# Seven-product attention: order of combine and denominators, place of one maximum, of the statistics and of the filling work

## Chip, cores and metric

The kernel runs on one core of a Trainium2 chip. The metric is device time in microseconds (us); a lower number is better. TensorE does the matmuls, VectorE (DVE in the profile), ScalarE (ACT) and GpSimd (POOL) the elementwise work, and SyncE (SP) starts most of the DMAs.

## What is computed

The input is four images of 256 channels and 64 x 64 pixels, in fp32. Two layers follow each other. The reference, cut to what matters:

```python
# layer 0: attention over the 4096 pixels of one image
q = wq @ x + bq            # 32 x 4096
k = wk @ x + bk            # 32 x 4096
v = wv @ x + bv            # 256 x 4096
attn = softmax(q.T @ k)    # 4096 x 4096, over the keys
x = gamma * (v @ attn.T) + x

# layer 1: cluster block, then MLP, then pointwise
y = x + ls1 * cluster(group_norm(x))   # 4 heads of 24, folds of 32 x 32, 4 centres each
y = y + ls2 * (W2 @ gelu(W1 @ group_norm(y)))          # 256 -> 1024 -> 256
z = relu(batch_norm(y * dw_w))
z = relu(batch_norm(pw_w @ z))
```

Group norm needs mean and variance over a whole image, and the cluster block needs sums of the attention's output over patches (the "cells").

## The kernel before, in words

**Stages.** The images go through one after the other: attention (some 495 us of an image's 800), cluster, MLP. Around them the work of the next image is interleaved: its projections, its first scores and the maxima of its first block of queries are made during the cluster block and the MLP of the image before. Only the first image has a stretch of its own for that, `alone` (L810), the prologue.

**Attention.** `weighting` (L880) goes over eight blocks of 512 queries; each block over eight units of 512 keys, so an image has 64 units, u = 8 nb + g. TensorE multiplies the 512 x 512 exponentials of a unit with v. In units g = 0 to 6 this is done with seven products in place of eight quarter products (`weigh`, L682: 28 matmuls of 128x256); the operands need sums of the four quarters of the exponentials (`factors`: VectorE makes t31 in L619, GpSimd the rest through `plus`, L598 and L614). Unit 7 is done plainly (L660). `weigh` is cut into four parts, and between the parts stand the pieces of other work: TensorE's order of work is thus written out by hand in this loop.

**Scores ahead.** `due` puts the scores of the unit eleven further on between the parts: two products (L423) into one buffer of two PSUM banks, a copy to SBUF (`kept`, ScalarE, L436) and a running maximum (`highest_of`, VectorE, L447), which reads the PSUM tile. There are two such buffers, but one of them holds the block's maximum and a part of the exponentials (`hold`) during the whole weighting. In a few places (`kept_only`, and the second half of a unit g = 0) the maximum isn't taken from PSUM but later from the SBUF copies: it is put into the list `held`, and `caught(n)` runs the first n of that list. In the trace the first kind reads `top<-sc,top`, the second `top<-s,top`.

**A unit on the other engines.** `exps(u+1)` subtracts the maximum (VectorE, L586, twice 128x1024) and takes exponentials (ScalarE, L591, L592, L595). `factors(u+1)` follows.

**End of a block.** With unit 7, `evict` copies the first two of the four accumulators out of PSUM (ScalarE, L702). `gather` sums the denominators (GpSimd, two additions of 128x256 into `rden`, L598). `combine` (L712 to L715) joins the copied quarters in four operations of 128x256; it runs on GpSimd in blocks 0 to 6 and on VectorE in block 7. `complete` (L727, VectorE) adds the other two accumulators to that, and only then may the next block's first matmul into them start. Later units of the next block do `total` (the denominators' reciprocal), `leave` (L751, the division, on GpSimd) and `sent` (DMA to a DRAM buffer). GpSimd's queue starts the DMAs that add the result to x (`back`, L775).

**Statistics.** Units 57 to 62 carry for each finished block two bn_stats (`seen`, L797) ahead of the first part of `weigh`, and the sum of the cells (`pooled`, L802) ahead of its third part, all on VectorE.

**Filling.** `cluster` (L1042) has many short dependent steps. Between them `fill(n)` pops n pieces from the list of the next image's projections: 32 halves of v (`v_half`, matmuls L378, ScalarE's copy L386) with four pieces for q and k among them (`halved`: matmuls, then two halves of the fp32 value made by ScalarE, L335, and VectorE, L336, and four stores each on SP's queue). `fill(N)` in `mlp` (L1842) takes all that are left, after the MLP's first piece.

Of the kernel before, what the change touches and what calls it, by code (L numbers as in the profile page):

```python
# [8 lines left out]
F32 = mybir.dt.float32  # L9
F32R = mybir.dt.float32r  # L10
# [4 lines left out]
P = 128  # L15
B, C, H, W = 4, 256, 64, 64
N = H * W
KC = C // P
NB = 512
NBLK = N // NB  # L20
# [9 lines left out]
RG, GRP = 4, N // NB  # L30
# [4 lines left out]
SEVEN = 7  # L35
# [18 lines left out]
def attention_then_cluster_block(  # L54
# [250 lines left out]
    def attention(b, xs, ys):  # L305
# [20 lines left out]
        def halves_of(which, i, hi, lo, ps, dma=nc.sync):  # L326

            col = 1 if which == "k" else 0
            if which not in own:
                own[which] = dram.tile([NBLK // RG, P, 4, NB], F32, tag=which, name=f"{which}_{b}")
            bias = bqk_s[:, col : col + 1]
            nc.scalar.activation(hi, ps, AF.Identity, bias=bias)  # L335
            nc.vector.scalar_tensor_tensor(  # L336
                lo, ps, bias, hi.bitcast(F32), ALU.add, ALU.subtract
            )
            rows = own[which][i]
            for c in range(4):  # L340
                part = hi if c in ((0, 2) if which == "k" else (0, 1)) else lo
                dma.dma_start(out=rows[:, c], in_=part.bitcast(F32))
# [16 lines left out]
        def halved(which, i):  # L359

            ps = ps_m.tile([P, NB], F32, tag="m", name=f"{which}p_{b}_{i}")
            parts = [
                big.tile([P, NB], F32R, tag="k", bufs=2, name=f"hl{j}_{which}_{b}_{i}")
                for j in range(2)
            ]
            projected(which, i, ps)
            halves_of(which, i, *parts, ps)

        vps = {}

# [17 lines left out]
        def v_pair(i):  # L388
            v_half(2 * i)
            v_half(2 * i + 1)  # L390
# [121 lines left out]
        def across(nb, tag="w2", tp=None):  # L512
            if tp is None:
                tp = turned_over(nb, ps_m.tile([P, 4, P], F32, tag="m", name=f"tt_{b}_{nb}"))
            mx = small.tile([P, 4], F32, tag="mx", name=f"mx_{b}_{nb}")
            nc.vector.tensor_reduce(mx, tp, AX.X, ALU.max)
            dg = work.tile([P, 4, P], F32, tag=tag, bufs=1, name=f"dg_{b}_{nb}")
            nc.vector.tensor_tensor(
                dg,
                ident.unsqueeze(1).to_broadcast([P, 4, P]),  # L520
                mx.unsqueeze(2).to_broadcast([P, 4, P]),
                ALU.mult,
            )
            return dg
# [267 lines left out]
                y = block(ys, k, nb).rearrange("p (h n) -> p h n", h=2)  # L792
                nc.vector.tensor_tensor(y, y, rows_of(t, k), ALU.add)

        def seen(nb):
            for c in range(KC):
                nc.vector.bn_stats(stats[:, 2 * nb + c, :], block(ys, c, nb))  # L797

        def pooled(nb):
# [12 lines left out]
        def alone():  # L812

            roots()
            for i in range(3):
                v_pair(i)
            staged("first", (("k", 0), ("q", 0)))
            k_unit(0)
            q_block(0)
            q_block(1)  # L820
            for i in range(3, 8):
                v_pair(i)
            for g in range(4):
                for f in sums(g):
                    f()
            for u in range(GRP):
                if u == 0:
                    begun(0)
                    staged("second", (("k", 1), ("q", 1)))
                    rest = load_rest()  # L830
                hooks, maxima = [], []
                score(u, hooks, maxima)
                for f in hooks + maxima:
                    f()
                v_pair(u + GRP)
                if u > 1:
                    next(rest, None)
            fold(0)
            for g in range(4, SEVEN):
                for f in sums(g):  # L840
                    f()
            dgs["dg"] = across(0)
            half(GRP, 0)
            spread(0, dgs["dg"])
            wf()
            half(GRP, 1)
            exps(0)
            factors(0)
# [32 lines left out]
        def weighting(next_x, fill, early, begin):  # L881
# [25 lines left out]
            for u in range(units):  # L907
                nb, g = divmod(u, GRP)
                more = nb + 1 < NBLK
                ripe = more and nb and g == 5  # L910

                short = nb == 0 and g == 6
                if g == 0:
                    done, av = av, [
                        pool.tile([P, NB], F32, tag=tag, name=f"av{c}_{b}_{nb}")
                        for c, (pool, tag) in enumerate(
                            ((ps_a, "a0"), (ps_a, "a1"), (ps_m, "m"), (ps_m, "m"))
                        )
                    ]
                maxima = due(u, 0)  # L920
                if g == GRP - 1:
                    gather(nb)
                if g == SEVEN:
                    evict(nb, av, 0)
                    evict(nb, av, 1)
                    combine(nb, nc.gpsimd if more else nc.vector)
                if g + 1 < GRP or more:
                    exps(u + 1)
                for f in maxima:
                    f()  # L930
                if nb < 2 or g == 3:
                    caught(1)

                if nb and g == 0:
                    complete(nb - 1, done, 1)
                elif nb and g == 1:
                    den = total(nb - 1)
                    next(den)
                elif nb and g == 2:
                    next(den)  # L940
                elif ripe:
                    peak = highest(nb + 1)
                    next(peak)
                if u == 0:
                    early()
                if u in views:
                    seen(views[u])
                if u in shifts:
                    shift(shifts[u])
                weigh(u, av, 0)  # L950
                if short:
                    two = ps_s.tile([P, 2, NB], F32, tag="s", name=f"tt_{b}_{nb + 1}")
                    tp = turned_over(nb + 1, two[:, 0].rearrange("p (j n) -> p j n", j=4))
                for f in due(u, 1):
                    f()
                weigh(u, av, 1)
                if short:
                    dgs["dg"] = across(nb + 1, "w2", tp)
                if g == GRP - 1 and not more:
                    complete(nb, av, 0)  # L960
                if u == units - 2:
                    back_one(NBLK - 2)
                maxima = due(u, 2)
                if more and nb and g == GRP - 2:
                    known(mb)
                if g + 1 < GRP or more:
                    factors(u + 1)
                if ripe:
                    next(peak)
                    mb = next(peak)  # L970
                for f in maxima:
                    f()
                if (u, 0) not in at or (u, 1) in at:
                    caught(1)
                if u in views:
                    pooled(views[u])
                weigh(u, av, 2)
                if short:
                    spread(nb + 1, dgs["dg"])
                for f in due(u, 3):  # L980
                    f()
                if nb and g == 1:
                    next(den)
                elif nb and g == (4 if more else 3):
                    leave(nb - 1)
                elif nb and g == (5 if more else 4):
                    sent(nb - 1)
                weigh(u, av, 3)
                if g == 3 and nb + 2 < NBLK:
                    q_block(nb + 2)  # L990
                if g == GRP - 1 and more:
                    complete(nb, av, 0)
                tail(u)
# [38 lines left out]
        parts.score, parts.fold, parts.q_block, parts.k_unit = score, fold, q_block, k_unit  # L1032
        parts.maximum, parts.first, parts.exps, parts.half = maximum, first, exps, half
        parts.projections = [lambda i=i: v_half(i) for i in range(N // P)]
        for i, f in (
            (27, lambda: halved("q", 1)),
            (20, lambda: halved("k", 1)),
            (14, lambda: halved("q", 0)),
            (13, lambda: halved("k", 0)),
        ):  # L1040
            parts.projections[i:i] = [f]
        return parts  # L1042


# [2 lines left out]
    def cluster(b, ys, stats, cells, rest, fill, gelu, nxt, maxima, turn):  # L1047
# [213 lines left out]
                        stop=(not first and j == 7),  # L1261
                    )

        fill(2)
        heads(NBLK - 1)
        similar(1)
        fill(2)
        summed(lambda j, q: pool_w[:, j], True)
        gelu(1)
        turn()  # L1270
        fill(4)
        table(AF.Sqrt)

        affine(0)
# [48 lines left out]
        )  # L1323
        g_s = work.tile([P, C], F32, tag="acc", bufs=1, name=f"g_{b}")
        nc.scalar.copy(g_s, gp[:, :C])
        fill(1)
        stats2 = small.tile([P, 2 * NBLK, 6], F32, tag="stats", name=f"st2_{b}")
        pieces = {}

# [59 lines left out]

        nxt.q_block(0)  # L1390
        nxt.k_unit(0)
        fill(4)
        copies = []
        nxt.score(0, copies, maxima)
        copies.pop()()
# [644 lines left out]
```

## Time and profile before

| | us |
|---|---|
| median of 3 runs | 3228.34 (3226.5 to 3228.45) |
| the profiled execution, its own time | 3225.25 |
| its span in the trace | 3223.3 |
| prologue, 0 to 74: TensorE busy | 51.99 of 74.00 |
| weighting of the first image, 74 to 569: TensorE busy | 477.94 of 495.00 |
| cluster of the first image, 569 to 633: TensorE busy | 57.08 of 64.00 |
| MLP of the first image, 633 to 870: TensorE busy | 234.83 of 237.00 |

The mean TensorE clock granted is 0.991 of full speed.

How to read the lines: an instruction or a group names its line in the code, engine, operation, and tiles as output<-inputs (buffer numbers left out) with partitions x elements. In the timeline a line begins with the start and the duration in us; in brackets at its end stands how long its engine was idle ahead of it and which instruction ended the idle time. In the list of groups the count is followed by the busy time, the mean duration of one in ns, and then the idle time ahead of the group's instructions with what ended it. In the list of waits each line has the waiting engine, its tile and line, then the one waited for, and the total, the number of times and the longest. A wait for several things is put down to the one that came last.

### The profile page before, as it was taken

How to read it: one execution, taken by the hardware profiler on the slowest of the kernel's cores; microseconds unless marked ns; L12 is line 12 of the kernel's file. 1: busy time of each engine (PE TensorE's matmuls, PEld its weight loads, DVE VectorE, ACT ScalarE, POOL GpSimd, SP SyncE). 2: the span in 40 equal slices, each digit the busy share in tenths (PEclk: the TensorE clock that was granted, in tenths of full speed). 3: DMA queues.
4: the chain of work that ended last, by engine and by line, in shares of the span. 5: the costliest groups of instructions: out<-in, count | busy, mean ns of one | idle time of the engine just before them, and what ended most of it. 6: DMA issues, size and time to landing. Idle time of an engine off the chain costs nothing.

```text
span 3223.3 us, 40475 instructions
## 1 busy us (share of the span) xinstructions
PE 3087.0 (96%) x13890; PEld 2444.0 (76%) x13890; DVE 2506.6 (78%) x3648; ACT 1732.9 (54%) x2719; POOL 2259.6 (70%) x2143
## 2 busy tenths in 40 slices
PE   7999999999999999999999999999999999998999
PEld 5777787688677787778867778776876787875786
DVE  4888887667788887777778888777778888877665
ACT  4556554545555656344555666544555556654444
POOL 4778787378488778647848878855766788783663
PEclk8999999999999999999999999999999999999999
DMA  5122116100112112510011211441011122150000
GB/s 163 40 63 63 54 58 188 63 20 30 46 50 63 53 60 87 160 50 21 30 56 43 63 60 58 112 126 50 30 43 43 53 59 63 56 142 7 14 20 27
DMA packets 105869, 200.33 MB, mean 62 GB/s; under 512 B 14416, under 2 KB 30400, under 8 KB 104128
## 3 DMA queue, kind: packets, MB, share of 16 engines
q1 hardware_dynamic: 101856, 181.94, 17.7%
q0 software_dynamic: 2976, 14.70, 2.5%
q8 instruction: 110, 1.80, 0.2%
q10 hardware_dynamic: 832, 1.11, 0.1%
q14 instruction: 95, 0.78, 0.1%
HBM read 149.37 MB, written 48.34 MB: 61 GB/s over the span
## 4 chain that ended last, share of the span: by engine, by line
PE 46%; POOL 26%; DVE 15%; issue 6%; ACT 4%; DMA 2%; SPq 0%; POOLq 0%; ACTq 0%; DVEq 0%
PE mo L1652 10%; PE av L682 9%; POOL acc L598 8%; PE hq L1735 5%; DVE top L447 4%; POOL t L598 4%; POOL acc L614 4%; POOL s L598 4%; DVE s L586 3%; PE sc L423 3%; PE hp L1735 3%; PE hr L1735 3%; PE fv L1226 3%; DVE t L619 2%; PE vp L378 2%
## 5 line engine op out<-in xcount | busy, mean ns | idle before, releaser
L436 ACT COPY s<-sc 128x1024 f32<-128x1024 f32 x512 | 513.9, 1010 | 514.4 <-PE sc L423 510.0
L586 DVE TENSOR_TENSOR s<-s,hold 128x1024 f32<-128x1024 f32 x512 | 598.8, 1210 | 29.4 <-ACT hold L569 15.7
L598 POOL TENSOR_TENSOR s<-t,s 128x512 f32<-128x512 f32 x224 | 303.5, 1355 | 391.5 <-DVE t L619 323.0
L682 PE MATMUL av<-t,v 128*128 128x256 f32 x1792 | 463.1, 381 | 12.8 <-DVE t L619 11.6
L682 PE MATMUL av<-s,v 128*128 128x256 f32 x1792 | 463.3, 381 | 12.4 <-DVE t L727 10.3
L682 PE MATMUL av<-s,sum 128*128 128x256 f32 x1792 | 461.8, 380 | 0.0
L598 POOL TENSOR_TENSOR acc<-acc,t 128x512 f32<-128x512 f32 x352 | 460.6, 1329 | 0.0
L423 PE MATMUL sc<-q,k 128*128 128x512 f32 x1024 | 402.8, 479 | 43.1 <-DVE top L447 17.5
L447 DVE TENSOR_TENSOR top<-sc,top 128x1024 f32<-128x1024 f32 x312 | 380.4, 1219 | 56.0 <-ACT s L436 53.1
L1690 ACT ACTIVATE hs<-hs,pv_s 128x256 f32<-128x256 f32 x496 | 232.3, 502 | 343.2 <-DVE hs L1726 343.2
L619 DVE TENSOR_TENSOR t<-s,hold 128x1024 f32<-128x1024 f32 x224 | 272.6, 1217 | 158.7 <-ACT s L595 97.6
L682 PEld LDWEIGHTS av<-s,v 128*128 128x128 f32 x1792 | 341.0, 191 | 69.8 <-issue 12.9
L682 PEld LDWEIGHTS av<-t,v 128*128 128x128 f32 x1792 | 339.5, 190 | 67.0 <-DVE t L619 18.2
L1652 PE MATMUL mo<-hs,w 128*128 128x256 f32 x1512 | 385.3, 381 | 0.0
L682 PEld LDWEIGHTS av<-s,sum 128*128 128x128 f32 x1792 | 341.1, 190 | 55.4 <-issue 1.9
L1652 PEld LDWEIGHTS mo<-hs,w 128*128 128x128 f32 x1512 | 283.1, 190 | 47.1 <-ACT hs L1690 6.4
L598 POOL TENSOR_TENSOR t<-s 128x512 f32<-128x512 f32 x224 | 295.9, 1321 | 17.6
L423 PEld LDWEIGHTS sc<-q,k 128*128 128x128 f32 x1024 | 177.0, 190 | 155.4 <-DVE top L447 82.1
L595 ACT ACTIVATE s<-s 128x1024 f32<-128x1024 f32 x256 | 267.5, 1045 | 1.2
L591 ACT ACTIVATE hold<-s 128x512 f32<-128x512 f32 x224 | 135.1, 603 | 246.3 <-DVE s L586 246.0
L1726 DVE TENSOR_TENSOR hs<-hq,hs 128x256 f32<-128x256 f32 x496 | 198.8, 422 | 78.9 <-PE hq L1735 69.0
L682 PE MATMUL av<-t,sum 128*128 128x256 f32 x896 | 230.8, 380 | 0.0
(299 smaller groups left out, 5325.1 us busy)
## 6 DMA issues: line engine op xcount, KB each, us to landing
k<-k SPq DMA_DIRECT2D x256, 256.0 KB, 2.7
x<-in_x SPq DMA_DIRECT2D x62, 512.0 KB, 6.7
out<-xn SPq DMA_DIRECT2D x62, 256.0 KB, 2.1
att<-t SPq DMA_DIRECT2D x56, 256.0 KB, 3.9
x<-att POOLq DMA_DIRECT2D x12, 1024.0 KB, 8.3
q<-q SPq DMA_DIRECT2D x32, 256.0 KB, 4.1
w<-in_w SPq DMA_DIRECT2D x8, 1024.0 KB, 9.6
rden<-row_rd SPq DMA_DIRECT2D x28, 256.0 KB, 3.7
```

Of the source, the lines that this page charges most:

```text
L423: nc.tensor.matmul(sc[:, r, :], k_s[:, (2 * h + r) * P : (2 * h + r + 1) * P], qs[u // GRP], start=True, stop=True,)
L436: nc.scalar.copy(slots[u][:, PAIR[h]].rearrange("p h r n -> p r h n"), tiles(sc))
L447: nc.vector.tensor_tensor(top, src, top if saved[nb] is None else saved[nb], ALU.max)
L586: nc.vector.tensor_tensor(sh, sh, mb.to_broadcast([P, 2, 2, QW]), ALU.subtract)
L595: nc.scalar.activation(s[:, PAIR[1]], s[:, PAIR[1]], AF.Exp)
L598: nc.gpsimd.tensor_tensor(out, x, y, op)
L619: nc.vector.tensor_tensor(t31[u], s[:, B11 : B22 + 1 : 2], b12.to_broadcast([P, 2, 2, QW]), ALU.add)
L682: nc.tensor.matmul(av[bank][:, half_ * QW : (half_ + 1) * QW], a[:, r], t[:, r], start=(g == 0 and r == 0 and i in (1, 7, 2, 4)), stop=(g ...
L1652: return nc.tensor.matmul(bank[:, half * HB : (half + 1) * HB], a[:, j], t, start=start, stop=stop)
L1690: nc.scalar.activation(src, src, AF.Gelu_apprx_tanh, bias=pvc("b1", P, j + 4 * (i > 1)))
L1726: nc.vector.tensor_tensor(dst, ps, term, ALU.add)
L1735: nc.tensor.matmul(out, w, x, start=True, stop=True)
```

## The change

It has six parts.

1. In unit 7, `combine` stands ahead of `gather` in blocks 0 to 5. Both stay on GpSimd.
2. In block 6 `combine` moves from GpSimd to VectorE, and in blocks 6 and 7 it comes after `exps(u + 1)`.
3. `caught(1)` at the third unit (g = 3) of the later blocks is now at g = 6. The list is a queue, so the maximum is taken in the block before the one in which it was taken: at u = 22, 30, 38 and 46.
4. In units 57 to 62 the cells and one of the two bn_stats stand ahead of the first part of `weigh`, the other bn_stats stands ahead of the third part.
5. In the prologue the maxima are taken as in `half` (128x1024, from PSUM; one from SBUF) and no longer in four operations of 128x512 a unit from SBUF; v pairs 14 and 15 move behind the transposes of the maximum and the start of unit 8's scores.
6. In the filling, the pieces k1 and q1 move to the end of the list; the counts of `fill` change so that four more halves of v stand ahead of `agg`, none between `gp` and the `op` products, one in place of four ahead of the next image's first score, and the rest (with k1 and q1) in the MLP's `fill(N)`. The last image, which has no next one, keeps its counts. The two tiles of a `halved` piece are one tile of `work` with the tag of t31, in place of two of the k buffers.

The diff:

```diff
@@ halved
             ps = ps_m.tile([P, NB], F32, tag="m", name=f"{which}p_{b}_{i}")
-            parts = [
-                big.tile([P, NB], F32R, tag="k", bufs=2, name=f"hl{j}_{which}_{b}_{i}")
-                for j in range(2)
-            ]
+            two = work.tile([P, 2, NB], F32R, tag="t13", name=f"hl_{which}_{b}_{i}")
             projected(which, i, ps)
-            halves_of(which, i, *parts, ps)
+            halves_of(which, i, two[:, 0], two[:, 1], ps)
@@ seen
-        def seen(nb):
-            for c in range(KC):
+        def seen(nb, cs=range(KC)):
+            for c in cs:
                 nc.vector.bn_stats(stats[:, 2 * nb + c, :], block(ys, c, nb))
@@ alone
-                hooks, maxima = [], []
-                score(u, hooks, maxima)
-                for f in hooks + maxima:
-                    f()
-                v_pair(u + GRP)
+                for h in range(2):
+                    half(u, h)()
+                caught(1)
+                if u < 6:
+                    v_pair(u + GRP)
...
-            dgs["dg"] = across(0)
+            tp = turned_over(0, ps_m.tile([P, 4, P], F32, tag="m", name=f"tt_{b}_0"))
             half(GRP, 0)
+            v_pair(14)
+            dgs["dg"] = across(0, "w2", tp)
             spread(0, dgs["dg"])
+            v_pair(15)
             wf()
@@ weighting
                 maxima = due(u, 0)
-                if g == GRP - 1:
-                    gather(nb)
                 if g == SEVEN:
                     evict(nb, av, 0)
                     evict(nb, av, 1)
-                    combine(nb, nc.gpsimd if more else nc.vector)
+                    if nb < NBLK - 2:
+                        combine(nb, nc.gpsimd)
+                    gather(nb)
                 if g + 1 < GRP or more:
                     exps(u + 1)
+                if g == SEVEN and nb >= NBLK - 2:
+                    combine(nb, nc.vector)
                 for f in maxima:
                     f()
-                if nb < 2 or g == 3:
+                if nb < 2 or g == 6:
                     caught(1)
...
                 if u in views:
-                    seen(views[u])
+                    pooled(views[u])
+                    seen(views[u], (0,))
...
                 if u in views:
-                    pooled(views[u])
+                    seen(views[u], (1,))
                 weigh(u, av, 2)
@@ the list of projections
-        for i, f in (
-            (27, lambda: halved("q", 1)),
-            (20, lambda: halved("k", 1)),
-            (14, lambda: halved("q", 0)),
-            (13, lambda: halved("k", 0)),
-        ):
-            parts.projections[i:i] = [f]
+        parts.projections[14:14] = [lambda: halved("q", 0)]
+        parts.projections[13:13] = [lambda: halved("k", 0)]
+        parts.projections += [lambda: halved("k", 1), lambda: halved("q", 1)]
@@ cluster
-        fill(2)
+        fill(4 if nxt else 2)
         heads(NBLK - 1)
         similar(1)
-        fill(2)
+        fill(0 if nxt else 2)
         summed(lambda j, q: pool_w[:, j], True)
         gelu(1)
         turn()
-        fill(4)
+        fill(8 if nxt else 4)
...
         nc.scalar.copy(g_s, gp[:, :C])
-        fill(1)
+        fill(0 if nxt else 1)
...
         nxt.k_unit(0)
-        fill(4)
+        fill(1)
         copies = []
```

## Prediction

> **What bounds the kernel now.** I read the page's busy times first, then TensorE's waits, then the timeline around each wait that the diff touches.
>
> ```profile
> PE 3087.0 (96%) x13890; PEld 2444.0 (76%) x13890; DVE 2506.6 (78%) x3648; ACT 1732.9 (54%) x2719; POOL 2259.6 (70%) x2143
> ```
>
> TensorE bounds. The diff leaves its instructions as they are, so what can be won is idle time, plus stretches at a lower clock. My sum of its gaps is 132 us: weighting 15.5, 16.8, 14.8 and 16.5 in the four images, prologue 19.9, the rest outside. The waits say who is late:
>
> ```profile
> PE sc L423 <- DVE top L447: 17.5, 31, 1.4
> PE av L682 <- DVE t L619: 11.6, 18, 1.2
> PE av L682 <- DVE t L727: 11.3, 5, 2.6
> PE tt L509 <- DVE top L504: 7.8, 2, 6.3
> PE agg L1256 <- DVE sim L1186: 7.5, 4, 2.0
> PE gnm_gn L276 <- DVE mv_gn L274: 7.0, 3, 2.3
> ```
>
> (Columns: total us, times, longest.) VectorE is the last link in all of them. What is VectorE waiting for? First the boundary between blocks 6 and 7, from the timeline:
>
> ```profile
> 491.92 1.22 DVE L619 TENSOR_TENSOR t<-s,hold 128x1024 f32<-128x1024 f32 x1 [2.28 <-ACT s L595]
> 492.86 1.71 POOL L598 TENSOR_TENSOR rden<-acc 128x256 f32<-128x256 f32 x2
> 494.23 1.00 POOL L712 TENSOR_TENSOR t<-t 128x256 f32<-128x256 f32 x1
> 496.91 0.72 POOL L715 TENSOR_TENSOR t<-t 128x256 f32<-128x256 f32 x1
> 497.67 0.75 DVE L727 SCALAR_TENSOR_TENSOR t<-av,pv_s,t 128x512 f32<-128x512 f32 x1 [4.53 <-POOL t L715]
> 498.57 2.04 PE L682 MATMUL av<-s,v 128*128 128x256 f32 x4 [2.60 <-DVE t L727]
> ```
>
> GpSimd forms the denominators (two rden), then combines the quarters (four operations, 3.4 us); VectorE's complete stands idle 4.53 us for that, and TensorE 2.60 us for complete. Over all blocks it is the same link:
>
> ```profile
> L727 DVE SCALAR_TENSOR_TENSOR t<-av,pv_s,t 128x512 f32<-128x512 f32 x32 | 24.0, 751 | 38.3 <-POOL t L715 37.9
> ```
>
> 37.9 us of idle VectorE before 28 completes: 4.5 to 4.8 in block 6, about 0.8 in most of the others. Then the units that carry the statistics, 60 to 62:
>
> ```profile
> 524.81 2.34 DVE L586 TENSOR_TENSOR s<-s,hold 128x1024 f32<-128x1024 f32 x2
> 527.07 1.28 DVE L797 BATCH_NORM_STATS2 st<-x 128x6 f32<-128x512 f32 x2
> 529.43 1.22 DVE L619 TENSOR_TENSOR t<-s,hold 128x1024 f32<-128x1024 f32 x1 [1.08 <-POOL acc L598]
> 530.57 1.21 DVE L802 TENSOR_REDUCE cells<-x 128x8 f32<-128x1024 f32 x1
> 530.70 1.13 PE L682 MATMUL av<-t,v 128*128 128x256 f32 x4 [0.58 <-DVE t L619]
> 531.70 2.34 DVE L586 TENSOR_TENSOR s<-s,hold 128x1024 f32<-128x1024 f32 x2
> ```
>
> One turn takes 531.70-524.81 = 6.89 us, and TensorE waits 0.58 in each: its own unit is 28 matmuls x 0.216 = 6.05. VectorE idles 1.08 before t and then does cells after it, where the next turn needs it.
>
> **What the Trainium skill says.** "SBUF — State Buffer", section "SBUF: two separate sides": VectorE and GpSimd share a port pair; a VectorE operation with two SBUF inputs and a GpSimd operation on SBUF exclude each other for a whole instruction. The trace agrees:
>
> ```profile
> 149.45 1.72 DVE L447 TENSOR_TENSOR top<-s,top 128x1024 f32<-128x1024 f32 x1
> 150.05 2.26 POOL L598 TENSOR_TENSOR acc<-acc,t 128x512 f32<-128x512 f32 x1
> ```
>
> 1.72 against 1.22 us for the same maximum alone, 2.26 against 1.27 for the addition. "PSUM — Partial Sum Buffer", section "PSUM bank collisions raise a hardware error": two engines may not access one bank at once. A maximum read from PSUM thus follows ScalarE's copy of that tile; at 252.75 it waits 2.03 us for the copy. "TensorE: Matmul & The Clock Gate", Part 1 "The HAM clock gate": after an idle window of about 3.4 us matmuls run at half rate for about as long. Here, after the 2.60 us gap at 498.57, 16 matmuls took 0.43 us each, not 0.22, which is 1.6 us more; image 1's 2.56 us gap cost nothing further.
>
> **Part 1: block 6, combine on VectorE; statistics moved.** The four operations leave GpSimd (3.4 us) and come to VectorE. In block 7 they run there already, at 0.41 alone and 0.83 beside GpSimd: 1.7 us free of GpSimd, 2.5 to 3.3 with it. They stand behind the subtractions (end 489.64) and the copies out of PSUM (489.45), so ahead of t of unit 56, which ended at 493.14. With the lock I put their end at 493.9, t at 495.0 and complete at 495.7, against 498.4 before. What is queued behind them on VectorE is t and with it TensorE's second term: about 1.0 us of the 2.60 gap stays there.
>
> The tail from there runs on VectorE's turn. After the change cells and one bn_stats lie under ScalarE's exponentials, the other bn_stats (0.60) follows t. A turn is 4.62 (start of the subtractions to t, ScalarE's chain) + 1.14 + 0.60 = 6.36, against 6.89; TensorE's 6.05 stays below. VectorE's own work there, 2.25 + 1.13 + 0.60 = 3.98, fits under the 4.62. Following both through, TensorE's term 5 of unit 62 comes at 533.6, not 537.59: 4.0 us, and 0.2 at the end, where 0.60 stands before combine in place of 1.13. So **4.2 us an image, 16.8 for four**. Bounds: 3.0 if the lock costs its whole measure and the half-clock stretch stays, 5.8 if there is no lock and no half clock: 12 to 23.
>
> **Part 2: blocks 0 to 5, combine ahead of rden on GpSimd.** Same six operations, other order: combine ends 1.43 us earlier (494.23 less 492.86, with the change of operation). ScalarE's copies end before the last acc, so nothing else is late. rden's reader, the denominators' reduction, is a unit away. TensorE's gaps in unit 0 of the next block are what this can fill; I read them block by block:
> - boundaries 0 and 1: 0.65+1.50, 0.63+1.07, 0.61+1.27, 0.61+0.16; each capped at 1.43 makes 6.4 us.
> - boundaries 2 to 5: gaps of 0.66 .87 .49 .63, .45 .11 .53 1.14, .54 .29 .33 .59, 0 0 .65 .79. Here part 3 takes back about 1.0 of the 1.43, so at most 0.43 each: 1.7+1.3+1.55+0.86 = 5.4.
>
> Sum 11.8; I take **10.5**, since the next late thing there (the k loads in unit 6, 1.8 to 5.2 us an image, which this doesn't touch) may eat a little. Bounds 3 and 14.4 (all the gaps, if the lock costs nothing).
>
> **Part 3: the SBUF maximum in the seventh unit.** The maximum of two SBUF tiles, 1.53 us, moves from unit 3 to unit 6 of blocks 2 to 5, 16 times in all. Unit 6 prepares unit 7, which has no t31, and VectorE idles 2.03 us there before its second maximum: 1.53 fits. Its DVE price is nothing; if that cover were gone, 1.5. But GpSimd had 1.8 to 1.9 us of slack in unit 3 and none at the block's end, so the lock's 1.0 falls on combine: counted in part 2. What unit 3 frees was hidden. **0**.
>
> **Part 4: prologue.** Fourteen maxima of 128x1024 from PSUM (1.22 each) and one from SBUF replace thirty of 128x512 (12 of them took 11.38 us). VectorE comes out of its backlog (the 6.30 us in front of the transposes falls to some 5), but a PSUM bank must now pass product, copy and maximum in turn (0.70+1.01+1.22 and the handovers, about 3.25, against a unit of 2.65), and unit 0's exponentials now come after v pair 15. **0**; from -1.5 to +2 (minus is a gain).
>
> **Part 5: filling.** Four more halves of v (3.46 us) stand before agg, k1 and q1 (1.85+1.86) no longer before op and the first score. agg is bound by VectorE's sim at 605.31 either way. Then op and group norm come earlier: 629.00 becomes about 626.4, since hl_k and hl_q (0.67+0.65) leave VectorE's queue. In exchange 3.71-1.73 = 1.98 us of TensorE work stand after the first hp: 0.6 net, three times. But the longer idle (about 4 us) ahead of gnm invites the half clock, which costs 0.8 to 1.3. On SP's queue q_0, k_0 and k_1 now pass the stores of k1 and q1, which only helps. **0**; -3 to +2.
>
> **Sum.** 3225.25 (profiled execution: span 3223.3 and 1.95 around it) - 16.8 - 10.5 = 3197.9. The median of the runs shown is 3.09 above that execution; I carry that over: **3201**.
>
> **Rivals.**
> - *The freed waits come back at the next late thing* (k loads, PSUM's one score buffer): part 2 gives about 3, part 1 about 14. 3228.3-17 = 3211. For it: the 13.8 us on k loads and image 3's zero gaps at two boundaries; against it: those loads lie six units on.
> - *The lock hardly bites and half-clock stretches go:* part 1 22, part 2 14.4, part 5 +1: 3191. For it: all four 6-to-7 gaps fall below the 2.5 us after which three of four slowed.
> - *No measurable change*, 3225: the combine only takes VectorE's place as late link. Against it: 4.53 us of idle VectorE is wider than the 1.7 to 3.3 that come.
> - *Slower:* the SBUF maximum in unit 6 under the lock. If it delays the second maximum there, the single free score buffer comes late and TensorE waits: 1.53 + 1.0 = 2.5 us at each of 16 places, 40 us, and blocks 2 to 5 lose their 5.4 of part 2: 3201+45 = 3246. It decides once the idle before that maximum (2.03) is shorter than maximum and lock; 1.72 as measured under the lock is still below.
>
> **Chances.** Forecast 0.56, come-back 0.16, less lock 0.14, no change 0.06, slower 0.08. About 0.2% (6.5 us) is what a measurement of this kernel can tell from no change; three cases lie beyond it: faster 0.86, same 0.06, slower 0.08. The forecast's own bounds are 3195 to 3207; the range goes on to the two neighbours and their unknowns, 3189 to 3214, and leaves out the last two cases.
>
> **What would show it.** Right: the idle before complete in block 6 falls from 4.5 to under 1.5, the timeline at block 7's units 60 to 62 turns in about 6.4 with gaps under 0.3, VectorE's idle behind GpSimd's combine falls from 37.9 to under 12, and the waits for L447 hardly change. Wrong: SBUF maxima near 1.7 us with TensorE waits behind them in unit 6, the gap ahead of the transposes not smaller, or half-clock stretches ahead of the first hp in all images.

## The result, and the profile after

| | before | changed |
|---|---|---|
| median, us | 3228.25 (3226.5 to 3228.45, 4 runs) | 3199.15 (3196.98 to 3200.63, 4 runs) |
| profiled execution, us | 3225.25 | 3196.98 |
| its span, us | 3223.3 | 3195.0 |

The ratio is 0.9911, 95% interval 0.9893 to 0.9928: 0.9% faster. The forecast was 3201. The total came out; the parts of the sum didn't, as the table below shows.

The page of the changed kernel (its lines are numbered up to three lower: L447 is L444, L619 is L616, L682 is L679, L715 is L712, L727 is L724):

```profile
PE 3085.5 (97%) x13890; PEld 2445.7 (77%) x13890; DVE 2537.0 (79%) x3649; ACT 1734.8 (54%) x2719; POOL 2260.6 (71%) x2127
```

TensorE is busy as long as before; the gain is idle time (27.3 of the 28.3 us by which the span is shorter). From its list of waits:

```profile
PE gnm_gn L276 <- DVE mv_gn L274: 12.8, 3, 4.3
PE av L679 <- DVE t L616: 11.7, 8, 2.2
PE sc L420 <- DVE top L444: 10.2, 21, 1.0
PE tt L506 <- DVE top L501: 4.7, 2, 3.2
PE agg L1255 <- DVE sim L1185: 2.4, 4, 1.6
```

The waits of the accumulators av for complete (11.3 us) have left the list, those for the maximum are down from 17.5, those for gnm are up from 7.0. The group of complete itself:

```profile
L724 DVE SCALAR_TENSOR_TENSOR t<-av,pv_s,t 128x512 f32<-128x512 f32 x32 | 23.9, 747 | 5.3 <-POOL t L712 4.3 <-DVE t L712 0.5
```

VectorE's idle time ahead of it fell from 38.3 to 5.3 us. The boundary between blocks 6 and 7 in the first image, from the timeline:

```profile
482.99 0.58 DVE L709 TENSOR_TENSOR t<-t 128x256 f32<-128x256 f32 x1
483.60 1.38 DVE L710 TENSOR_TENSOR t<-t 128x256 f32<-128x256 f32 x1
485.02 1.38 DVE L711 TENSOR_TENSOR t<-t 128x256 f32<-128x256 f32 x1
486.06 0.97 POOL L772 DMA_DIRECT2D x<-att  x1
486.43 2.33 DVE L712 TENSOR_TENSOR t<-t 128x256 f32<-128x256 f32 x1
486.74 1.74 POOL L595 TENSOR_TENSOR rden<-acc 128x256 f32<-128x256 f32 x2
488.69 1.21 DVE L616 TENSOR_TENSOR t<-s,hold 128x1024 f32<-128x1024 f32 x1
489.82 0.74 DVE L724 SCALAR_TENSOR_TENSOR t<-av,pv_s,t 128x512 f32<-128x512 f32 x1
489.95 1.97 PE L679 MATMUL av<-t,v 128*128 128x256 f32 x4 [2.20 <-DVE t L616]
```

Complete no longer waits, but combine takes 5.77 us on VectorE (482.99 to 488.76), more than the 2.5 to 3.3 that the forecast allowed beside GpSimd, and t31 stands behind it: TensorE's gap is still 2.20 us, now for t31. And the tail, on VectorE:

```profile
524.60 1.21 DVE L799 TENSOR_REDUCE cells<-x 128x8 f32<-128x1024 f32 x1
525.73 0.69 DVE L794 BATCH_NORM_STATS2 st<-x 128x6 f32<-128x512 f32 x1
526.97 1.22 DVE L616 TENSOR_TENSOR t<-s,hold 128x1024 f32<-128x1024 f32 x1 [0.55 <-POOL acc L595]
528.11 0.69 DVE L794 BATCH_NORM_STATS2 st<-x 128x6 f32<-128x512 f32 x1
```

From the cells of one unit to the next (the next is at 530.96) it is 6.36 us, as forecast. (t31 is the operation that the lines show as `t<-s,hold`.)

**Where the time came from.** For each unit I took the time from its first weighting matmul to that of the next, in both traces, and summed the differences over the four images (minus is a loss):

| stretch | forecast, us | measured, us |
|---|---|---|
| unit 0 of blocks 1 to 6 (behind complete; the prediction's parts 2 and 3) | 10.5 | 14.9 |
| unit 3 of blocks 1 to 6 (its part 3) | 0 | 4.5 |
| unit 6 of blocks 1 to 6 (k loads) | 0 | 1.3 |
| block 7 (its part 1), 2.86 to 2.90 an image | 16.8 | 11.5 |
| block 0 | 0 | 0.6 |
| all of weighting | 27.3 | 32.7 |
| all outside of weighting (prologue, cluster, MLP) | 0 | -4.4 |
| the span | 27.3 | 28.3 |

### The profile page after: what moved, and what is told of

The parts are those of the page before. It is cut to its first block, busy times and chain, and to the rows that moved or that the text cites. A ratio compares the mean times of both kernels' runs of the same rounds, so it can differ in the third digit from the quotient of the medians.

```text
span 3195.0 us, 40473 instructions
## 1 busy us (share of the span) xinstructions
PE 3085.5 (97%) x13890; PEld 2445.7 (77%) x13890; DVE 2537.0 (79%) x3649; ACT 1734.8 (54%) x2719; POOL 2260.6 (71%) x2127
## 4 chain that ended last, share of the span: by engine, by line
PE 42%; POOL 24%; DVE 19%; issue 8%; ACT 6%; DMA 1%; POOLq 0%; SPq 0%; ACTq 0%; DVEq 0%
PE mo L1651 10%; POOL acc L595 9%; PE av L679 6%; PE hq L1734 5%; DVE top L444 5%; DVE s L583 4%; POOL t L595 4%; POOL s L595 4%; DVE t L616 3%; PE hp L1734 3%; PE hr L1734 3%; PE fv L1225 3%; PE sc L420 3%; POOL acc L611 2%; PE vp L375 2%
## 5 line engine op out<-in xcount | busy, mean ns | idle before, releaser
L679 PE MATMUL av<-t,v 128*128 128x256 f32 x1792 | 464.8, 382 | 12.8 <-DVE t L616 11.7
L679 PE MATMUL av<-s,v 128*128 128x256 f32 x1792 | 460.8, 379 | 2.2 <-ACT s L589 2.2
L679 PE MATMUL av<-s,sum 128*128 128x256 f32 x1792 | 459.5, 379 | 0.0
L420 PE MATMUL sc<-q,k 128*128 128x512 f32 x1024 | 405.6, 480 | 36.8 <-DMA k<-k 10.5
L444 DVE TENSOR_TENSOR top<-sc,top 128x1024 f32<-128x1024 f32 x326 | 397.8, 1220 | 29.7 <-ACT s L433 24.8
L616 DVE TENSOR_TENSOR t<-s,hold 128x1024 f32<-128x1024 f32 x224 | 272.7, 1217 | 159.3 <-ACT s L592 71.0
L679 PEld LDWEIGHTS av<-t,v 128*128 128x128 f32 x1792 | 338.4, 190 | 70.1 <-DVE t L616 21.4
L679 PEld LDWEIGHTS av<-s,v 128*128 128x128 f32 x1792 | 340.3, 190 | 57.8 <-ACT s L589 2.6
L679 PEld LDWEIGHTS av<-s,sum 128*128 128x128 f32 x1792 | 339.4, 189 | 54.5 <-issue 1.9
L679 PE MATMUL av<-t,sum 128*128 128x256 f32 x896 | 231.7, 381 | 0.0
```

The costliest lines, as they stand in the source:

```text
L420: nc.tensor.matmul(sc[:, r, :], k_s[:, (2 * h + r) * P : (2 * h + r + 1) * P], qs[u // GRP], start=True, stop=True,)
L444: nc.vector.tensor_tensor(top, src, top if saved[nb] is None else saved[nb], ALU.max)
L616: nc.vector.tensor_tensor(t31[u], s[:, B11 : B22 + 1 : 2], b12.to_broadcast([P, 2, 2, QW]), ALU.add)
L679: nc.tensor.matmul(av[bank][:, half_ * QW : (half_ + 1) * QW], a[:, r], t[:, r], start=(g == 0 and r == 0 and i in (1, 7, 2, 4)), stop=(g ...
```

## The experiments

Theory: the order on GpSimd is the larger part of the gain; block 7's gain comes from VectorE's chain there; the moved maximum and the prologue are worth nothing; the moved filling costs. Rivals: the gain of blocks 0 to 6 belongs to the moved maximum; combine's move to VectorE is what matters in block 7. The kernels' medians, against 3227 to 3228.3 for the kernel before beside them (single runs of one kernel lie up to 8.5 us apart, so a difference of less than about 2 us between two of these medians tells nothing; the traces say more):

| kernel | median, us | ratio to before, 95% interval |
|---|---|---|
| order_alone | 3208.65 | 0.9938, 0.9925 to 0.9950 |
| no_maximum | 3198.98 | 0.9907, 0.9892 to 0.9922 |
| no_filling | 3201.0 | 0.9919, 0.9905 to 0.9933 |
| no_prologue | 3197.82 | 0.9906, 0.9892 to 0.9919 |
| pool_six | 3199.36 | 0.9910, 0.9896 to 0.9923 |
| split_six | 3203.01 | 0.9922, 0.9908 to 0.9935 |
| no_stats | 3205.87 | 0.9931, 0.9919 to 0.9944 |
| stats_first | 3197.15 | 0.9903, 0.9889 to 0.9916 |
| early_k1 | 3196.25 | 0.9904, 0.9889 to 0.9919 |
| back_later | 3194.79 | 0.9896, 0.9881 to 0.9911 |
| together | 3190.8 | 0.9887, 0.9870 to 0.9903 |

**The order alone.** On the kernel before:

```diff
-                if g == GRP - 1:
-                    gather(nb)
                 if g == SEVEN:
                     evict(nb, av, 0)
                     evict(nb, av, 1)
-                    combine(nb, nc.gpsimd if more else nc.vector)
+                    if nb < NBLK - 2:
+                        combine(nb, nc.gpsimd)
+                    gather(nb)
+                    if nb >= NBLK - 2:
+                        combine(nb, nc.gpsimd if more else nc.vector)
```

> The kernel before with one edit: combine ahead of the denominators on GpSimd in blocks 0 to 5 (block 6 as before). Theory (the order alone does it): TensorE's gaps in unit 0 after blocks 0 to 5 fall from 14.6 us in all to about 2.7, and the time falls by more than that, 13 to 17 us (3228 to about 3213), because a matmul's recorded end overlaps the next start by 0.16 us, so a gap hides 0.16 more than it shows. Rival (the moved maximum or the other parts gave a share of what blocks 0 to 6 gained): 5 to 10 us here, 3218 to 3223, with gaps of 1 us and more left at some boundaries.

Measured: 18.4 us faster by the medians (3227.04 to 3208.65), 19.6 by the spans. Unit 0 of blocks 1 to 6 is 19.8 us shorter in the trace; the other units of these blocks and block 7 are the same within 0.4 us, block 0 is 1.3 shorter. TensorE's gaps there fell from 14.6 to 0.9: that is 13.7, a third less than the time won. One boundary shows why. Before, then order_alone, TensorE's timeline at the second scores of block 3's unit 0:

```profile
265.32 1.03 PE L682 MATMUL av<-s,v 128*128 128x256 f32 x4
266.87 0.72 PE L423 MATMUL sc<-q,k 128*128 128x512 f32 x2 [0.53 <-DVE top L447]
```

```profile
261.72 1.03 PE L682 MATMUL av<-s,v 128*128 128x256 f32 x4
262.40 0.81 PE L423 MATMUL sc<-q,k 128*128 128x512 f32 x2
```

From start to start it is 1.55 us with the wait and 0.68 without: the wait costs 0.87, and the trace shows 0.53 idle, because the recorded end of the matmuls ahead (262.75) reaches 0.35 us past the start of the scores, where nothing is waited for. So the theory's direction holds, but my 0.16 a gap was too small, and 13 to 17 too little. Also, the wait that vanished is one for the maximum (17.5 us of such waits before, 6.1 here): complete was late, and the maximum stands behind it in VectorE's order of work.

**The maximum back in the third unit.** On the changed kernel:

```diff
-                if nb < 2 or g == 6:
+                if nb < 2 or g == 3:
                     caught(1)
```

> The changed kernel with the SBUF maximum of blocks 4 to 7 back in the third unit. Theory (it doesn't matter: combine on GpSimd took 3.15 us with the maximum in the seventh unit as it did before without): within 2 us of the changed kernel, 3197 to 3201, and the idle times before complete after blocks 2 to 5 stay between -0.1 and 0.5. Rival 1 (the forecast's lock, 1.0 us on GpSimd at each of 16 block ends): accumulations of block ends 1.0 earlier, 2 to 4 us faster, about 3196. Rival 2 (the third unit was short of VectorE, so the move is a gain): 3 us slower or more, with new gaps behind the maximum in unit 3.

Measured: 3198.98, the same. But "it doesn't matter" hides two effects that cancel: in the trace unit 0 of blocks 1 to 6 is 5.6 us shorter without the move, unit 3 is 4.8 us longer. Of the 4.8, 4.0 lie in the 16 places from which the maximum was moved (7.25 us a unit, 7.00 with the move), although the gaps shown in unit 3 differ by only 0.9 in all. The lock (the mutual exclusion of VectorE and GpSimd that the prediction prices) is seen in unit 6. The changed kernel, then no_maximum:

```profile
247.12 2.08 DVE L444 TENSOR_TENSOR top<-s,top 128x1024 f32<-128x1024 f32 x1
248.20 2.14 POOL L595 TENSOR_TENSOR acc<-acc 128x512 f32<-128x512 f32 x1
```

```profile
252.25 1.27 POOL L595 TENSOR_TENSOR acc<-acc 128x512 f32<-128x512 f32 x1
253.17 1.22 DVE L444 TENSOR_TENSOR top<-sc,top 128x1024 f32<-128x1024 f32 x1 [2.03 <-ACT s L433]
```

GpSimd's operation takes 0.87 us more with the maximum beside it, and the idle time ahead of all completes is 5.3 us with the move and this without:

```profile
L724 DVE SCALAR_TENSOR_TENSOR t<-av,pv_s,t 128x512 f32<-128x512 f32 x32 | 23.8, 742 | 1.2 <-DVE t L712 0.5 <-POOL t L712 0.3
```

Rival 1 (the lock reaches the block's end) and rival 2 (unit 3 gains) were both right, each by about 0.3 us a place.

The same lines answer the prediction's rival *Slower*. The SBUF maximum takes 2.08 us in unit 6, more than the 2.03 of idle time there, so by the prediction's own test the 40 us should have come. But the second maximum starts only 0.19 us later within its unit than in the kernel before (at 5.33 and not 5.15 us, the same in all 16 places), and TensorE's waits for it are unchanged (1.8 us in unit 6 of blocks 1 to 6, before and after): what counts is by how much the room is exceeded, not the whole of maximum and lock.

**The filling undone** (list, counts and tiles of part 6 as before).

> The changed kernel with part 6 undone (pieces, counts and tiles of the filling as before). Theory (the moved filling loses: gnm comes 2.2 us earlier than before but is preceded by 4.3 us of idle, after which matmuls run at half rate up to the first hp, and 2 us of work stand behind it): 3 to 5 us faster than the changed kernel, about 3195; stretch from the last hp of the cluster to the next image's weighting 1 to 1.7 us shorter in each of three images, gap ahead of gnm back at 2.3. Rival (the filling pays for itself, as the earlier agg says): 3199 to 3204.

Measured: 3201.0, 1.9 us slower than the changed kernel, with intervals that overlap: the theory, which wanted it faster, fell, and nothing more can be told from the medians. The trace shows a trade. In its lines and below, fv is the cluster's first product, gnm the mean of the second group norm, hp the MLP's first product. Changed kernel, first image:

```profile
617.43 0.59 PE L276 MATMUL gnm_gn<-mv_gn,left 128*128 128x1 f32 x2 [4.26 <-DVE mv_gn L274]
...
618.31 2.05 PE L375 MATMUL vp<-wv_s,x 128*128 128x256 f32 x4
...
620.44 3.33 PE L375 MATMUL vp<-wv_s,x 128*128 128x256 f32 x8
```

The same pieces in the kernel before:

```profile
629.47 1.11 PE L378 MATMUL vp<-wv_s,x 128*128 128x256 f32 x4
...
630.56 1.97 PE L378 MATMUL vp<-wv_s,x 128*128 128x256 f32 x8
```

From the first fv to gnm it is 58.05 us (559.38 to 617.43) where it was 60.22: 2.2 won. But the pieces behind gnm run at half rate, so gnm to hp is 6.2 and not 3.7 us, and k1 and q1 stand behind hp. With the old filling the half rate comes there too, in some images: fv to hp is 63.9, 66.1 and 63.9 us in the kernel before, 66.6, 65.3 and 63.9 in order_alone, 66.7, 66.0 and 66.8 in no_filling; with the new one it lies between 63.4 and 64.6 in eight profiles, while the stretch from hp to the next weighting is 1.0 to 2.3 us longer than before. Behind the 2.34 us gap of the old filling the half rate came in 6 of 9 places, behind the 4.26 of the new one in all 24. So the old filling was lucky in the profiled execution before (1 of 3 places); against no_filling, fv to the next weighting is 0.4, 0.6 and 0.5 us shorter in the changed kernel.

**The prologue undone** (part 5 as before).

> The changed kernel with part 5 undone (the prologue's maxima and v pairs as before). Theory (the gap ahead of the transposes is 3 us shorter in the changed kernel, but unit 0 then waits for its exponentials, so the first weighting starts no earlier): within 2 us of the changed kernel, 3197 to 3201, weighting of the first image starting at 73.5 to 76.5 as in both. Rival (the prologue's part is a gain of the size of that gap): 3 us slower, 3202.

Measured: 3197.82, the same. The changed kernel, then no_prologue:

```profile
63.87 1.09 PE L506 MATMUL tt<-ident,top 128*128 128x128 f32 x4 [3.23 <-DVE top L501]
...
73.75 2.08 PE L679 MATMUL av<-s,v 128*128 128x256 f32 x4 [2.15 <-ACT s L589]
```

```profile
66.29 1.08 PE L506 MATMUL tt<-ident,top 128*128 128x128 f32 x4 [6.85 <-DVE top L501]
...
74.93 1.13 PE L679 MATMUL av<-s,v 128*128 128x256 f32 x4 [2.15 <-ACT s L589]
```

The gap of 6.85 falls to 3.23, but from the transposes to the first weighting it is 9.88 us, not 8.64, as v pairs 14 and 15 lie there now. The start of weighting varies more than that: 73.4 to 76.8 us over the profiles with the new prologue; with the old one it is 73.9, 73.9 and 74.9.

**Block 6's combine on GpSimd, ahead of the denominators.**

```diff
-                    if nb < NBLK - 2:
+                    if more:
                         combine(nb, nc.gpsimd)
...
-                if g == SEVEN and nb >= NBLK - 2:
+                if g == SEVEN and not more:
                     combine(nb, nc.vector)
```

> The changed kernel with block 6's combine on GpSimd again, but ahead of the denominators, as in blocks 0 to 5. Theory (on VectorE it costs 5.8 us under the lock and holds up t31 of unit 56; on GpSimd it starts after the sums and the start of a DMA, near 1 us, and holds up only complete): gap between blocks 6 and 7 falls from 2.2 to about 1.3 us, 2 to 5 us faster, about 3196. Rival (VectorE is the right place: GpSimd ends 1.4 us earlier than in the kernel before but still late): gap 2.2 to 2.6 with a stretch at half rate after it, 3200 to 3207.

Measured: 3199.36, no change, though the gap did change its kind. GpSimd and complete:

```profile
488.67 0.94 POOL L772 DMA_DIRECT2D x<-att  x1
489.34 1.03 POOL L709 TENSOR_TENSOR t<-t 128x256 f32<-128x256 f32 x1
...
492.82 0.75 DVE L724 SCALAR_TENSOR_TENSOR t<-av,pv_s,t 128x512 f32<-128x512 f32 x1 [3.55 <-POOL t L712]
```

t31 of unit 56 is no longer held up, but complete ends no earlier, and block 7 keeps its length to 0.02 us. What sets that length is seen when the ends of t31 in units 57 to 62 are counted from block 7's start (second image; counted from the recorded end of the matmul ahead, which lies 0.16 us behind the start of block 7's first, to the recorded end of its last):

| kernel | t31 of units 57 ... 62 ends at, us | block 7, us |
|---|---|---|
| before | 10.71, 16.63, 23.46, 30.35, 37.23, 44.12 | 56.50 |
| changed | 9.37, 15.82, 22.16, 28.52, 34.88, 41.23 | 53.60 |
| pool_six | 9.37, 15.82, 22.17, 28.52, 34.87, 41.23 | 53.60 |
| no_stats | 9.37, 15.29, 22.12, 29.01, 35.90, 42.79 | 55.16 |
| stats_first | 9.36, 16.40, 22.74, 28.50, 34.27, 40.03 | 53.55 |
| back_later, third image | 8.47, 14.92, 21.27, 27.62, 33.98, 40.33 | 52.70 |

Complete, unit 57's subtractions, exponentials, t31, and then one turn a unit: TensorE's gap at the boundary lies beside that chain. The half rate behind the gap does too: in the changed kernel the first image has it early in block 7 (unit 57 starts at 10.04) and the second hasn't (8.60), and both end at 53.6 to 53.7.

**Combine cut in two around t31** (two of the four operations after `factors(u + 1)` in block 6).

```diff
-                    combine(nb, nc.vector)
+                    combine(nb, nc.vector, (0,) if more else (0, 1))
...
                     factors(u + 1)
+                if g == SEVEN and nb == NBLK - 2:
+                    combine(nb, nc.vector, (1,))
```

> The changed kernel with block 6's combine still on VectorE, but cut in two: two operations where all four stand, the other two after t31 of unit 56. Theory (the four operations under the lock, 5.8 us, hold t31 back by some 3 us, and TensorE's 2.2 us gap is the wait for it; complete comes only a little earlier, and the tail behind it follows VectorE): gap for t31 goes, one of 0.5 to 1.2 ahead of the term that needs complete takes its place, block 7 shorter by 0.3 to 0.9, 1 to 4 us faster than the changed kernel, 3195 to 3198. Rival (the gap alone counts): all of the 1.7 to 2.2 us an image, 3190 to 3192. Other rival (TensorE has slack behind it): no change.

Measured: 3203.01, 4 us slower: no theory had that. Timeline of the boundary:

```profile
487.69 1.22 DVE L616 TENSOR_TENSOR t<-s,hold 128x1024 f32<-128x1024 f32 x1
488.66 0.97 POOL L775 DMA_DIRECT2D x<-att  x1
488.83 3.75 DVE L714 TENSOR_TENSOR t<-t 128x256 f32<-128x256 f32 x1
489.34 1.73 POOL L595 TENSOR_TENSOR rden<-acc 128x256 f32<-128x256 f32 x2
490.71 1.57 POOL L595 TENSOR_TENSOR s<-t,s 128x512 f32<-128x512 f32 x1
...
494.98 1.16 PE L679 MATMUL av<-s,v 128*128 128x256 f32 x4 [2.97 <-DVE t L727]
```

One operation that takes 0.41 us alone took 3.75: it stood while GpSimd ran a DMA start and three operations back to back. Putting combine later put it into a stretch in which GpSimd has no pause. Block 7 is longer by 1.7, 0.3, 0.3 and 1.7 us in the four images, which makes the 4.

**The statistics back** (two bn_stats first, cells third, in units 57 to 62).

> The changed kernel with part 4 undone (two bn_stats ahead of the first part, cells ahead of the third). Theory (the tail runs on VectorE's turn): the turn of units 58 to 62 goes back from 6.36 to 6.89 us, TensorE's gaps of 0.58 in units 60 to 62 return, block 7 is 1.7 to 3 us longer than 53.6 in each image, 7 to 11 us slower than the changed kernel, 3206 to 3210. Rival (block 7's gain came from combine leaving GpSimd): block 7 at most 1 us longer, 3199 to 3203.

Measured: 3205.87, 6.7 us slower, just short of the forecast's lower bound; block 7 at 55.16 is 1.56 us longer, 6.2 for four, and the gaps of 0.58 are back. So a bit over half of block 7's 2.88 is the order of the statistics; the rest is the 1.3 us by which t31 of unit 57 is earlier.

**All statistics ahead of t31.**

```diff
-                    seen(views[u], (0,))
+                    seen(views[u])
...
-                if u in views:
-                    seen(views[u], (1,))
```

> The changed kernel with the second bn_stats of units 57 to 62 also ahead of the first part, so that nothing stands behind t31 there. Theory (turn = ScalarE's chain 4.62 + 1.14 + what follows t31; 2.25+1.13+0.60+0.60 = 4.58 still fits under the chain): turn falls from 6.36 to 5.8, TensorE's 6.05 becomes the bound, block 7 is 1.0 to 1.9 us shorter in each image, 4 to 7 us faster than the changed kernel, 3192 to 3195. Rival (TensorE bounds the tail already at 6.36, since its gaps are 0.05): within 2 us, 3198 to 3200.

Measured: 3197.15, block 7 unchanged: the forecast gain didn't come. The turn does fall to 5.77 (table), from unit 60 on. But unit 57 also carries a step of the denominators' reduction (transpose and reduction, 0.70 + 0.69 on VectorE), so nothing there was free under the exponentials, and t31 of unit 58 ends 0.6 later. TensorE waits for it:

```profile
507.85 1.13 PE L679 MATMUL av<-t,v 128*128 128x256 f32 x4 [0.73 <-DVE t L616]
```

From there TensorE works on without a gap of 0.1 us; units 60 and 62 take 6.04 us, its own time for 28 matmuls. So the 0.6 lost is just won back, and that t31 of unit 62 ends 1.2 us earlier isn't used. The rival was wrong that 6.36 is TensorE's bound, but TensorE is the bound once the turn has fallen below 6.04.

**The next late things.** k1's products ahead of the score:

```diff
-        parts.projections += [lambda: halved("k", 1), lambda: halved("q", 1)]
+        parts.projections[31:31] = [
+            lambda: own.update(k1=halved("k", 1, True)),
+            lambda: own["k1"](),
+        ]
+        parts.projections += [lambda: halved("q", 1)]
...
-        fill(1)
+        fill(2)
```

(`halved` with True returns the making of the halves, which `group_norm` runs after bn_aggr.)

> The changed kernel with the products of the piece k1 (1.9 us of TensorE) ahead of the next image's first score, and its two halves made after the second group norm's mean and variance are started. Theory (what the moved filling costs is the 4.3 us of empty TensorE ahead of gnm and the work put off behind the first hp): gap ahead of gnm 4.3 to about 2.3, the stretch from fv to the next weighting 2 us shorter in each of three images, 4 to 7 us faster than the changed kernel, 3192 to 3195; up to 3190 if the stretch at half rate behind the gap goes too. Rival (the chain on VectorE is disturbed, or the half-rate stretch comes anyway and longer): within 2 us, 3197 to 3201.

Measured: 3196.25, 2.9 us faster by the medians, with runs that overlap, and below what was expected. The 1.9 us filled a gap of 1.33 ahead of the second scores, and only 0.46 of the gap ahead of gnm (3.80 left); the half rate stayed. In the profiled executions the stretch from fv to the next weighting is 0.1 us longer in the first image and 0.6 and 1.0 shorter in the other two, not 2 in each.

Block 6's combine on GpSimd as in pool_six, and the accumulating DMA's start behind it:

```diff
-                    (units - 10, lambda: (load(2), back(0))),
+                    (units - 10, lambda: load(2)),
...
                         combine(nb, nc.gpsimd)
+                    if nb == NBLK - 2:
+                        back(0)
                     gather(nb)
```

> The changed kernel with block 6's combine on GpSimd, ahead of the denominators, and the first accumulating DMA's start (1 us of GpSimd) behind it and not in front. Theory (block 7 hangs on the chain complete of block 6, subtractions and exponentials of unit 57, t31, and then a turn of 6.36 a unit; combine without the lock and without the DMA start in front ends some 1 us earlier): complete and t31 of unit 57 about 1 us earlier than in the changed kernel, t31 ending at 8.2 to 8.7 after the block's start and not at 9.4, block 7 about 52.7 and not 53.6, 3 to 4 us faster than the changed kernel, 3195 to 3196. Rival (GpSimd is late with unit 57's operands then): no gain, 3198 to 3201.

Measured: 3194.79, 4.4 us faster than the changed kernel, as the chain foretold: t31 of unit 57 at 8.47 and block 7 at 52.7 in two images, 53.2 and 53.3 in the other two, where the half rate behind the boundary now shows (in the second image TensorE then runs every unit from 57 to 62 at its own 6.04, so it is the bound there).

Both edits, and the second bn_stats ahead of t31 in units 59 to 62 only:

> The changed kernel with both edits (k1's products early, block 6's combine on GpSimd with the DMA start behind it), and the second bn_stats ahead of the first part in units 59 to 62 only, where no step of the denominators stands. Theory: the gains add: 5 for k1, 3 to 4 for block 6, and, since the turn of units 60 to 62 falls below TensorE's 6.05, 0.6 to 1 an image, 2 to 4, for the statistics; 3185 to 3190. Rival (each gives its time to the next late thing): 3192 to 3196.

Measured: 3190.8 (3190.22 to 3192.97), faster than both kernels, 8.4 us below the changed one, and between theory and rival: the medians of block 6 and k1 add up (4.4 and 2.9), the statistics add nothing that can be seen. Block 7 is 52.65 at best, as with back_later alone. In the third image, for one, unit 60 does run at nearly TensorE's own time (6.09), but unit 61 takes 6.63: TensorE waits 0.22 us there, and nearly 0.4 from start to start, for an operand that GpSimd makes (`t`, L599), as it does in the first and the fourth. That is the next late thing.

## Why the prediction was right, and where only the sum was

*Bound and first link:* right. Nearly all of the gain is TensorE's idle time, and the idle time ahead of complete, 38.3 to 5.3, was where to look.

*Part 2:* right in mechanism, mis-sized. The term "TensorE's gaps in unit 0 ... are what this can fill", capped block by block, was 11.8 with the lock's price taken off, 10.5 taken; the order alone brought 19.8, and 14.9 stood with the maximum moved. Shown gaps were taken for the price of the waits; start to start a wait costs up to 0.35 us more. "Waits for L447 hardly change" failed for the same boundary: they were the symptom of complete's lateness, and fell with it. The upper bound of 14.4 was thus too low. (Two of the terms of its sum are slightly off as well: 1.3 and 1.55 should read 1.40 and 1.48.)

*Part 3:* "0" held as a sum (no_maximum), but not by its terms. The lock costs GpSimd 0.87, near the 1.0 that was put, but reaches the block's end with only about 0.3 (5.6 us over 16 places and not 16); and "what unit 3 frees was hidden" was wrong by 4.0 to 4.8 us. That the two nearly cancel is luck.

*Part 1:* 11.5, not 16.8, below its lower bound of 12. Two terms failed. Combine "under the lock" took 5.77 us and not up to 3.3, so t31 and complete came about 1.4 us after the forecast's 495.0 and 495.7 in relation to the subtractions; that is the 1.3 us an image that block 7 lacks. And the half rate behind the gap, part of the upper bound, wasn't on the path of block 7 in this kernel. The turns (6.36) and the vanished gaps of 0.58 were right. That combine should leave GpSimd at all was not needed: pool_six is as fast.

(The prediction counted 16 matmuls at half rate behind the 2.60 us gap. The trace has eight, and eight fit its 1.6 us.)

*Part 4:* 0, confirmed by no_prologue.

*Part 5:* 0, within its bounds by experiment (no_filling 1.9 slower). But one of its signs of being wrong came true: with the changed kernel's filling there is a half-rate stretch ahead of the first hp in all three images that have a next one. In the two profiled executions the stretches outside weighting are 4.4 us longer after; part of that is where half-rate stretches fell. 1.8 of it lies between the third image's last weighting matmul and its fv, where a half-rate stretch follows a gap of 1.54 us; images 1 and 2 have none at that place. How much is the filling's own is not settled, since old and new filling differ by less than that scatter.

So 27.3 came out as 28.3 because two waits that were priced too low (part 2, unit 3) and one stretch priced too high (part 1), with the loss outside, cancelled. The direction and the main cause were foreseen; that the sum came within 1 us is luck.

## What to carry to other kernels

When two engines run a chain in turn, put the operation that another engine waits for ahead of the one that nobody waits for: this order alone was worth two thirds of the gain. Price a wait from start to start against an undisturbed instance, not by the gap that the profile shows. Before moving work to an engine with idle time, check what shares a port with it in just that stretch, and which chain sets the end of the stage: a gap beside that chain is worth nothing.

## What was not expected of the hardware

A VectorE operation on two SBUF operands that meets a row of GpSimd operations without a pause can be delayed by more than one of them. The 1.38 us that it took in place of 0.41 can be a wait for a single addition of 1.27, but 2.33 and 3.75 are longer than any one of GpSimd's operations beside it. The start of a DMA on GpSimd need not be what holds it: in split_six's second image the third operation of combine took 0.42 us while such a start ran, and the fourth, beside the three operations after it, 3.30. And TensorE's half rate followed idle stretches of 1.5 to 4.3 us in some images and not in others at the same place: behind the 2.20 us gap of the changed kernel in the first image, not behind the 2.14 us gap of the second; behind 1.54 us ahead of v's matmuls at the end of the third image's attention; and behind 4.26 us ahead of gnm each time. So gaps shorter than the idle window of about 3.4 us that the prediction quotes can bring it, and not all of them do.
